# Group statistics of a second layer: from bn_stats on VectorE to accumulated activations on the scalar engine

## The chip, the cores and the metric

The kernel runs on one NeuronCore of one Trainium2 chip. The metric is the device time of one launch in microseconds; lower is better. Before the change three runs gave 3018.94 us at the median (3016.51 to 3023.95).

## The reference

The input x has 32 images of 32 channels of 128 x 128 numbers in fp32. Two layers run one after the other:

```
x = x + L0(gn(x))        # L0: matrix square root of each 128x128 channel, 5 Newton-Schulz steps
x = x + L1(gn(x), w1, w2)  # L1: 2-D Fourier transform, 32x32 low modes top and bottom
                           #     mixed over channels with w1 and w2, inverse transform, real part

def gn(v, G=16, eps=1e-5):     # per image and group of two channels
    g = v.reshape(B, G, C // G, H, W)
    m = mean(g, axis=(2, 3, 4)); s = var(g, axis=(2, 3, 4))
    return (g - m) / sqrt(s + eps)
```

The change touches the second gn alone: the mean and the variance of layer 1's input, over two channels of one image, 2 x 128 x 128 numbers. A Fourier transform is linear, so the kernel does not normalize layer 1's input. It transforms the raw values, multiplies the spectrum by 1 / sqrt(variance + eps), and corrects the one coefficient at frequency zero by the mean. So the statistics are needed only when an image's spectrum is finished.

## The kernel before

All data are fp32. The unit of work in layer 0 is a group of four channels of one image, a tile of 128 rows by 4 x 128 columns; an image has eight such groups, the launch 256. The square root of a channel is computed by a chain of matrix products on TensorE with short steps between them: VectorE combines a product with a tile, the scalar engine (ACT) copies or scales products out of PSUM, and GpSimd (POOL) subtracts from a scaled identity. There are two forms of the chain, "far" for images 1 to 18 and "near" for image 0 and images 19 to 31. The far form transposes on VectorE and puts the blocks together by four small DMAs from SyncE's queue; the near form transposes on TensorE.

The main loop counts rounds. In each round it visits eight lanes. A lane holds one group, written as a Python generator (`newton`); each visit runs the generator to its next `yield`, and so writes a few instructions into the engines' queues. A pause is a `yield` with no instruction. Nothing reorders what is written: the class `InOrder` keeps each engine's instructions in program order, so a round of the loop is a stretch of every engine's queue at once. A new group enters a free lane every 23/8 rounds in the far form and every 5 rounds in the near form. Next to the lanes there are queues of generators of which one step is taken at one place of each round: `norms` (scaling the input of coming groups), `preps` (layer 0's statistics of coming images, through `bn_stats`), `specs` (an image's layer 1 statistics and spectrum), `posts` (what follows a finished group), `prods` and `backs` (mixing products and inverse transforms of layer 1, for 20, 7, 3 and 2 images at a time). `posts` gets its step after the fourth lane. `step` works on the head of a queue, and when the head is exhausted goes on to the next at once.

A finished group is in the tile xt. `end` then appends `settle` to `posts`. `settle` stores xt to DRAM (`mid`), lets POOL fold its columns into a sum and a difference (tile fold), and takes the statistics of each pair of channels with VectorE's bn_stats, all in one step. After every four groups `forward` transforms the folded tiles on TensorE into u. After an image's eighth group `summed` is put on `specs`, and `spectrum` after it, so the second begins when the first has ended.

`bn_stats` writes six numbers for each partition, with a mean and a sum of squares about it for each of two halves. `summed` gets the group's statistics from these by way of `moments`: VectorE adds the half means, TensorE multiplies by avg_mean (a 128 x 128 matrix of one value, which sums over partitions and hands the sum to each of them), VectorE takes the differences from that mean, squares them and adds the rest. What comes out, two numbers for each of 16 groups, is widened from groups to channels (b_wide). Then four products with a 128 x 1 column avg_v sum it over partitions, each putting the 32 channels' variances on another 32 partitions of one PSUM tile, and a fifth gives the mean. A square root on ACT and one Newton step on VectorE give r, the factor by which ACT scales the spectrum.

PSUM has one pool of eight tiles (`bank`), taken in turn. xt has 14 buffers while the early ones exist, later 10; fold has three. ACT also issues the DMAs that load x, in two layouts, and the tiles for layer 0's statistics. Since every operation goes through a recording helper, the profile names line 89 for all of them, and its groups are told apart by their tiles.

Of the kernel before, what the change touches and what calls it, by code (L numbers as in the profile page):

```python
# [29 lines left out]
F32 = mybir.dt.float32  # L30
AF = mybir.ActivationFunctionType
ALU = mybir.AluOpType
AX = mybir.AxisListType
# [3 lines left out]
P = 128  # L37
B = 32
C = 32
G = 16  # L40
# [20 lines left out]
EPS = 1e-5  # L61
# [33 lines left out]
def conv_preact_kernel(  # L95
# [9 lines left out]
    nc = InOrder(tc)  # L105

    const = ctx.enter_context(tc.tile_pool(name="const", bufs=1))
# [10 lines left out]
    for n, f in (("v", EYE_V), ("q", EYE_Q)):  # L118
        e = const.tile([P, 1, P], F32, name=f"eye_{n}")
# [6 lines left out]
    avg_v = const.tile([P, 1], F32, name="avg_v")  # L126
    nc.vector.memset(avg_v, 0.5 / (P * P))
    avg_0 = const.tile([P, 1], F32, name="avg_0")
    nc.vector.memset(avg_0, -P * P / 256)


    mid = [dram.tile([P, C, P], F32, name=f"mid{b}", tag=f"mid{b}") for b in range(B)]
# [66 lines left out]
    def moments(st, ms, tag):  # L199

        n = st.shape[1]
        f = st.rearrange("p g (e t) -> p g e t", t=3)
        nc.vector.tensor_reduce(ms, f[:, :, :, 1], AX.X, ALU.add)
        yield from pause
        pm = bank()[:, 0, 0:n]
        nc.tensor.matmul(pm, avg_mean, ms, start=True, stop=True)
        nm = small.tile([P, n], F32, tag=f"{tag}_nm", name=f"{tag}_nm", bufs=2)
        nc.vector.tensor_scalar_mul(nm, pm, 2.0)
        d = small.tile([P, n, 2], F32, tag=f"{tag}_d", name=f"{tag}_d")
        nc.vector.tensor_tensor(  # L210
            d, f[:, :, :, 1], nm[:, :, None].to_broadcast([P, n, 2]), ALU.add
        )
        nc.vector.tensor_mul(d, d, d)
        nc.vector.scalar_tensor_tensor(d, d, 128.0, f[:, :, :, 2], ALU.mult, ALU.add)
        return nm, d
# [267 lines left out]
    def settle(b, g, st, xt):  # L483

        kept(nc.sync.dma_start(out=mid[b][:, 4 * g : 4 * g + 4, :], in_=xt))
        if g % 2 == 0:
            folds[b, g // 2] = sets.tile([P, 8, P], F32, tag="fold", name=f"fold{b}_{g}", bufs=3)
        f = folds[b, g // 2][:, 4 * (g % 2) : 4 * (g % 2) + 4, :]
        for half, op in enumerate((ALU.add, ALU.subtract)):
            nc.gpsimd.tensor_tensor(  # L490
                f[:, :, 64 * half : 64 * half + 64], xt[:, :, 0:64], xt[:, :, 64:128], op
            )
        for j in range(2):
            at = 8 * (g // 2 % 2) + 4 * (g // 4) + 2 * (g % 2) + j
            nc.vector.bn_stats(
                st[:, at, :], xt[:, 2 * j : 2 * j + 2, :].rearrange("p c h -> p (c h)")
            )
        settled.append(rounds)
        yield
# [35 lines left out]

    def summed(b, st):

        mq = small.tile([P, 2, G], F32, tag="b_mq", name=f"b_mq{b}")
        _, d = yield from moments(st, mq[:, 0, :], "b")
        yield  # L540

        nc.vector.tensor_reduce(mq[:, 1, :], d, AX.X, ALU.add)
        wide = small.tile([P, 2, G, 2], F32, tag="b_wide", name=f"b_wide{b}")
        nc.vector.tensor_copy(wide, mq[:, :, :, None].to_broadcast([P, 2, G, 2]))
        wide = wide.rearrange("p k g c -> p k (g c)")
        yield from pause
        pv = bank()[:, 0, :]
        for i in range(4):
            rows = slice(C * i, C * i + C)
            nc.tensor.matmul(pv[rows, 0:1], wide[:, 1, :], avg_v, start=True, stop=True)  # L550
        nc.tensor.matmul(pv[0:C, 1:2], wide[:, 0, :], avg_0, start=True, stop=True)
        v = small.tile([P, 2], F32, tag="b_v", name=f"b_v{b}")
        nc.vector.tensor_scalar(v[:, 0:1], pv[:, 0:1], 1.0, EPS, ALU.mult, ALU.add)
        nc.vector.tensor_copy(v[0:C, 1:2], pv[0:C, 1:2])
        yield
        s = small.tile([P, 3], F32, tag="b_r", name=f"b_r{b}")
        nc.scalar.activation(s[:, 0:1], v[:, 0:1], AF.Sqrt)
        yield
        nc.vector.reciprocal(s[:, 1:2], s[:, 0:1])
        nc.vector.tensor_scalar(  # L560
            s[:, 2:3], v[:, 0:1], s[:, 1:2], s[:, 1:2], ALU.mult, ALU.mult
        )
        nc.vector.tensor_scalar(s[:, 2:3], s[:, 2:3], -0.5, 1.5, ALU.mult, ALU.add)
        r = small.tile([P, 1], F32, tag="b_inv", name=f"b_inv{b}")
        nc.vector.tensor_mul(r, s[:, 1:2], s[:, 2:3])
        scales[b] = v, r
        yield
# [425 lines left out]
    made = {}  # L993
# [34 lines left out]
    def end(b, g, xt):  # L1028

        if g == 0:  # L1030
            u = up.tile([P, 2, 8, 2, L], F32, tag="u", name=f"u{b}")
            st = small.tile([P, G, 6], F32, tag="b_st", name=f"b_st{b}", bufs=2)
            ended[b] = (u, st)
        u, st = ended[b]
        posts.append(settle(b, g, st, xt))
        if g == C // 4 - 1:
            posts.append(then(summed(b, st)))
        if g % 4 == 3:
            posts.append(forward(b, g // 4, u))
        if g == C // 4 - 1:  # L1040
            posts.append(last(b, u))
# [144 lines left out]
```

## Time and profile before

| | us |
|---|---|
| median of three runs | 3018.94 |
| the profiled execution | 3016.65 |
| its span, first to last instruction | 3014.7 |
| TensorE busy (matmul) | 2897.6 |
| VectorE busy | 2321.8 |
| POOL busy | 1995.8 |
| scalar engine busy | 1652.1 |
| bn_stats on xt, 512 of 413 ns | 189.6 |
| bn_stats for layer 0, 504 of 412 ns and 8 of 418 ns | 188.4 |
| granted TensorE clock, share of full speed | 0.987 |

The profile is of one execution. A row "A <- B" in the list of waits gives the time that engine A stood idle until B had finished something, how often, and the longest. In the table of stages each engine has its busy time in the stretch and the number of its instructions. PE is TensorE's matmul side and PEld its weight loads, which overlap; DVE is VectorE and SP is SyncE. An fp32 product shows as two records, so a group's four products are eight. Tiles are named without their buffer numbers: ps is PSUM, and the names in `settle` and `summed` appear as b_st, b_mq, b_d, b_nm, b_wide, b_v, b_r and b_inv.

### The profile page before, as it was taken

How to read it: one execution, taken by the hardware profiler on the slowest of the kernel's cores; microseconds unless marked ns; L12 is line 12 of the kernel's file. 1: busy time of each engine (PE TensorE's matmuls, PEld its weight loads, DVE VectorE, ACT ScalarE, POOL GpSimd, SP SyncE). 2: the span in 40 equal slices, each digit the busy share in tenths (PEclk: the TensorE clock that was granted, in tenths of full speed). 3: DMA queues.
4: the chain of work that ended last, by engine and by line, in shares of the span. 5: the costliest groups of instructions: out<-in, count | busy, mean ns of one | idle time of the engine just before them, and what ended most of it. 6: DMA issues, size and time to landing. Idle time of an engine off the chain costs nothing.

```text
span 3014.7 us, 73315 instructions
## 1 busy us (share of the span) xinstructions
PE 2897.6 (96%) x27112; PEld 2689.0 (89%) x27112; DVE 2321.8 (77%) x4262; ACT 1652.1 (55%) x4187; POOL 1995.8 (66%) x2308
## 2 busy tenths in 40 slices
PE   7999999999999999999999999999989999999995
PEld 7899999999999999999999889888878899888884
DVE  7778898989888888889876645777886767776564
ACT  4566666566565656566554445455544544665452
POOL 4676777777777767777765434787777763678352
PEclk9999999999999999999999999999999999999997
DMA  5465655556565656565633566777877737676576
GB/s 176 135 176 145 171 163 153 167 152 180 134 192 135 192 131 195 142 183 140 190 102 99 158 209 208 257 247 254 271 235 245 252 121 225 203 242 216 175 230 242
DMA packets 442482, 560.91 MB, mean 186 GB/s; under 512 B 99344, under 2 KB 260112, under 8 KB 442128
## 3 DMA queue, kind: packets, MB, share of 16 engines
q1 hardware_dynamic: 328512, 347.77, 38.7%
q10 hardware_dynamic: 113616, 208.45, 22.2%
q8 instruction: 218, 3.57, 0.5%
q14 instruction: 136, 1.11, 0.1%
HBM read 326.93 MB, written 153.62 MB: 159 GB/s over the span
## 4 chain that ended last, share of the span: by engine, by line
PE 71%; POOL 8%; DVE 7%; DMA 7%; issue 5%; SPq 1%; ACT 1%; ACTq 0%; POOLq 0%; DVEq 0%
PE ps L89 71%; POOL yt L89 3%; POOL r L89 2%; POOL x L89 1%; POOL fold L89 1%; DMA yt<-mid 1%; SPq L89 1%; DVE turn L89 1%; DVE root L89 1%; DMA w<-turn 1%; DMA out<-yt 1%; DVE v L89 1%; DVE yt L89 1%; DVE a_d L89 1%; DMA xs<-in_xs 1%
## 5 line engine op out<-in xcount | busy, mean ns | idle before, releaser
L89 PE MATMUL ps<-my,q 128*128 128x128 f32 (+1 forms) x4096 | 747.0, 330 | 16.6 <-DVE q L89 9.9
L89 PEld LDWEIGHTS ps<-my,q 128*128 128x128 f32 x4096 | 623.0, 192 | 67.7 <-issue 7.4
L89 PE MATMUL ps<-w,v 128*128 128x128 f32 x4096 | 555.4, 279 | 19.6 <-DVE w L89 15.3
L89 ACT ACTIVATE b<-b,a_off,a_sc 128x128 f32<-128x128 f32 x1024 | 469.7, 491 | 166.2 <-issue 57.0
L89 ACT ACTIVATE my<-ps 128x512 f32<-128x512 f32 x512 | 306.2, 599 | 428.3 <-PE ps L89 408.9
L89 POOL TENSOR_TENSOR fold<-xt 128x256 f32<-128x256 f32 x512 | 363.4, 731 | 261.5 <-DVE xt L89 248.9
L89 PEld LDWEIGHTS ps<-w,v 128*128 128x128 f32 x4096 | 502.9, 193 | 32.5 <-DVE w L89 13.9
L89 POOL TENSOR_TENSOR yt<-yt,d 128x512 f32<-128x512 f32 x244 | 306.5, 1279 | 223.2 <-ACT d L89 195.5
L89 ACT ACTIVATE t<-ps 128x256 f32<-128x256 f32 x512 | 192.0, 381 | 311.7 <-PE ps L89 298.4
L89 DVE STREAM_TRANSPOSE turn<-v 128x512 f32<-128x512 f32 x288 | 326.1, 1132 | 9.9
L89 POOL TENSOR_SCALAR x<-xt,a_nm,a_sc 128x128 f32<-128x128 f32 x736 | 321.4, 450 | 15.6 <-DVE a_sc L89 15.4
L89 POOL TENSOR_TENSOR mb<-eye_q,mb 128x512 f32<-128x512 f32 x144 | 184.0, 1278 | 197.8 <-ACT y L89 139.2
L89 ACT ACTIVATE y<-ps,a_t_s 128x128 f32<-128x128 f32 x1024 | 290.4, 374 | 0.0
L89 POOL TENSOR_TENSOR v<-eye_v,x 128x512 f32<-128x512 f32 x144 | 184.0, 1278 | 143.8 <-ACT x L89 136.7
L89 PE MATMUL ps<-q,t 128*128 128x128 f32 x2048 | 273.9, 277 | 4.3 <-ACT t L89 3.7
L89 PE MATMUL ps<-x,b 128*128 128x128 f32 x2048 | 277.7, 279 | 0.0
L89 PE MATMUL ps<-x,q 128*128 128x128 f32 x2048 | 274.7, 277 | 3.0 <-DVE w L89 2.0
L89 DVE SCALAR_TENSOR_TENSOR v<-ps,v 128x512 f32<-128x512 f32 x288 | 195.1, 678 | 104.5 <-PE ps L89 101.8
L89 PE MATMUL ps<-y,t 128*128 128x128 f32 x2048 | 274.5, 277 | 0.1
L89 PE MATMUL ps<-my,mb 128*128 128x128 f32 x2048 | 272.2, 276 | 0.0
L89 PEld LDWEIGHTS ps<-my,mb 128*128 128x128 f32 x2048 | 257.9, 192 | 9.6 <-issue 1.6
L89 PEld LDWEIGHTS ps<-x,q 128*128 128x128 f32 x2048 | 249.4, 192 | 14.1 <-issue 8.4
(131 smaller groups left out, 5074.9 us busy)
## 6 DMA issues: line engine op xcount, KB each, us to landing
w<-turn SPq DMA_DIRECT2D x1152, 64.0 KB
b<-in_x ACTq DMA_DIRECT2D x256, 256.0 KB
xt<-in_xt ACTq DMA_DIRECT2D x256, 256.0 KB
mid<-xt SPq DMA_DIRECT2D x256, 256.0 KB
yt<-mid SPq DMA_DIRECT2D x128, 512.0 KB
xs<-in_xs ACTq DMA_DIRECT2D x252, 256.0 KB
out<-yt SPq DMA_DIRECT2D x115, 512.0 KB
plain<-in_wk SPq DMA_DIRECT2D x34, 512.0 KB
```

The costliest lines, as they stand in the source:

```text
L89: return self.tc.keep_in_program_order(issue(*args, **kw))
```

## The change

The second layer's statistics are gathered in another way. Layer 0's mean of each group is known from `prep` (a_nm, its negative). For each pair of channels `settle` now runs two activations on ACT over the 128 x 256 numbers: a Copy whose accumulated output is their sum per partition, and a Square with layer 0's negative mean as bias, whose accumulated output is the sum of squares about that mean. Their elementwise results go to one tile, waste, that nobody reads. A `yield` stands between the two pairs, so `settle` takes two rounds instead of one. bn_stats on xt is gone.

`summed` no longer calls `moments`. It widens sums, squares and layer 0's mean to channels (three VectorE copies, two of them for the mean's order of groups). For each of the four blocks of 32 partitions TensorE makes three products: the squares with avg_v, and the sum with avg_v and the mean with avg_s accumulated into one column, which gives the distance between the new mean and layer 0's. A product with avg_0 gives the mean as before, with another constant. On channels VectorE then takes the square of that distance off the mean of squares and adds eps. From there on nothing differs. The product with avg_mean and one of the two pauses of `summed` go; the statistics tile is 128 x 2 x 16 instead of 128 x 16 x 6, and a_nm has three buffers instead of two, since `summed` reads it late. `moments` itself stays, for layer 0.

```diff
-    nc.vector.memset(avg_0, -P * P / 256)
+    nc.vector.memset(avg_0, -0.5)
+    avg_s = const.tile([P, 1], F32, name="avg_s")
+    nc.vector.memset(avg_s, 1 / P)
+    waste = const.tile([P, 2 * P], F32, name="waste")
...
-        nm = small.tile([P, n], F32, tag=f"{tag}_nm", name=f"{tag}_nm", bufs=2)
+        nm = small.tile([P, n], F32, tag=f"{tag}_nm", name=f"{tag}_nm", bufs=3)
...
+        at = 8 * (g // 2 % 2) + 4 * (g // 4) + 2 * (g % 2)
         for j in range(2):
-            at = 8 * (g // 2 % 2) + 4 * (g // 4) + 2 * (g % 2) + j
-            nc.vector.bn_stats(
-                st[:, at, :], xt[:, 2 * j : 2 * j + 2, :].rearrange("p c h -> p (c h)")
+            if j:
+                yield
+            of = xt[:, 2 * j : 2 * j + 2, :].rearrange("p c h -> p (c h)")
+            n = 2 * g + j
+            nc.scalar.activation(
+                waste, of, AF.Copy, accum_out=st[:, 0, at + j : at + j + 1]
+            )
+            nc.scalar.activation(
+                waste,
+                of,
+                AF.Square,
+                bias=made[b][0][:, n : n + 1],
+                accum_out=st[:, 1, at + j : at + j + 1],
             )
...
-        mq = small.tile([P, 2, G], F32, tag="b_mq", name=f"b_mq{b}")
-        _, d = yield from moments(st, mq[:, 0, :], "b")
-        yield
-
-        nc.vector.tensor_reduce(mq[:, 1, :], d, AX.X, ALU.add)
-        wide = small.tile([P, 2, G, 2], F32, tag="b_wide", name=f"b_wide{b}")
-        nc.vector.tensor_copy(wide, mq[:, :, :, None].to_broadcast([P, 2, G, 2]))
+        wide = small.tile([P, 3, G, 2], F32, tag="b_wide", name=f"b_wide{b}")
+        nc.vector.tensor_copy(wide[:, 0:2], st[:, :, :, None].to_broadcast([P, 2, G, 2]))
+        for half in range(2):
+            nm = made[b][0].rearrange("p (a h c) -> p h a c", a=2, h=2)[:, half]
+            nc.vector.tensor_copy(
+                wide[:, 2, 8 * half : 8 * half + 8].rearrange("p (a c) e -> p a c e", a=2),
+                nm[:, :, :, None].to_broadcast([P, 2, 4, 2]),
+            )
...
             nc.tensor.matmul(pv[rows, 0:1], wide[:, 1, :], avg_v, start=True, stop=True)
+            nc.tensor.matmul(pv[rows, 2:3], wide[:, 0, :], avg_v, start=True, stop=False)
+            nc.tensor.matmul(pv[rows, 2:3], wide[:, 2, :], avg_s, start=False, stop=True)
         nc.tensor.matmul(pv[0:C, 1:2], wide[:, 0, :], avg_0, start=True, stop=True)
-        v = small.tile([P, 2], F32, tag="b_v", name=f"b_v{b}")
-        nc.vector.tensor_scalar(v[:, 0:1], pv[:, 0:1], 1.0, EPS, ALU.mult, ALU.add)
+        v = small.tile([P, 4], F32, tag="b_v", name=f"b_v{b}")
+        nc.vector.tensor_copy(v[:, 2:3], pv[:, 2:3])
         nc.vector.tensor_copy(v[0:C, 1:2], pv[0:C, 1:2])
+        nc.vector.tensor_scalar(v[:, 3:4], v[:, 2:3], v[:, 2:3], -1.0, ALU.mult, ALU.mult)
+        nc.vector.tensor_scalar(v[:, 0:1], pv[:, 0:1], EPS, v[:, 3:4], ALU.add, ALU.add)
...
-            st = small.tile([P, G, 6], F32, tag="b_st", name=f"b_st{b}", bufs=2)
+            st = small.tile([P, 2, G], F32, tag="b_st", name=f"b_st{b}", bufs=2)
```

## The prediction

> **What bounds the kernel now.** I read the engine totals first, then the 40 slices, then busy time by stage, then who waits for whom on TensorE and on the scalar engine, and last the timeline round the places that the edit touches.
>
> From the page, the totals and three rows of slices:
>
> ```profile
> PE 2897.6 (96%) x27112; PEld 2689.0 (89%) x27112; DVE 2321.8 (77%) x4262; ACT 1652.1 (55%) x4187; POOL 1995.8 (66%) x2308
> ...
> PE   7999999999999999999999999999989999999995
> ...
> DVE  7778898989888888889876645777886767776564
> ACT  4566666566565656566554445455544544665452
> ```
>
> TensorE is full nearly everywhere; VectorE comes second, at eight to nine tenths in the first half. The same by stage (span, then PE, PEld, DVE, ACT, POOL busy, clock, DMA share, GB/s), once in the far stage (images 1 to 18) and once in the near stage:
>
> ```profile
> 700.00:1000.00 300.00, 298.50 (x2506) 282.96 (x2505) 259.38 (x456) 181.66 (x464) 217.28 (x239) 1.00 0.57 157
> ...
> 2000.00:2300.00 300.00, 284.34 (x2540) 255.88 (x2538) 234.25 (x417) 154.88 (x406) 228.31 (x262) 0.99 0.75 247
> ```
>
> In the far stage TensorE idles 1.5 of 300 us, in the near stage 15.7. So VectorE's 86% does not set the pace: what is taken from it can return only what TensorE waits for it. Those waits, over the whole span, are these (total, times, longest):
>
> ```profile
> PE ps L89 <- DVE w L89: 18.2, 12, 3.2
> PE ps L89 <- DVE a_ms L89: 11.5, 1, 11.5
> PE ps L89 <- DVE q L89: 11.2, 15, 5.1
> PE ps L89 <- ACT my L89: 9.3, 7, 4.1
> ...
> PE ps L89 <- DVE b_wide L89: 4.4, 5, 1.5
> PE ps L89 <- DVE a_d L89: 4.2, 9, 1.0
> PE ps L89 <- DVE b_mq L89: 3.8, 1, 3.8
> ```
>
> With the smaller rows of that answer (v 2.2, xt 1.1, b_st 0.8, yt 0.5, b_v 0.3) TensorE waits 58.2 us for VectorE. Of this the 11.5 us for a_ms is the first image's statistics, which stay; 46.7 us can be touched, and 9.0 of them (b_wide, b_mq, b_st) belong to the chain that is rewritten.
>
> The room on the engine that gets the work, in the far stage, from its waits between 700 and 1000 us:
>
> ```profile
> ACT my L89 <- PE ps L89: 52.0, 44, 3.6
> ACT t L89 <- PE ps L89: 25.4, 40, 1.5
> ACT mb L89 <- PE ps L89: 9.4, 11, 1.3
> ACT b L89 <- issue: 5.0, 14, 1.3
> ```
>
> With z (3.3) the scalar engine waits 90 us for TensorE: time that other work can fill. The other 28 us of its idle time hang on transfers that it issues and on other engines, and are not free. The stage finishes 29 groups of four channels in these 300 us (58 bn_stats on xt, two a group), one in 10.3 us; so a group leaves 3.1 us free there.
>
> **What the Trainium skill says.** "ScalarE: Activation LUTs", section "What ACT_TABLE_LOAD costs", prices an ACTIVATE at 186 ns + 0.833 ns an element with immediates and 280 ns with one pointer operand. The trace agrees: 128x256 copies out of PSUM (z) take 380 ns against 399, the 128x128 scaling with one pointer (y) 374 against 387. Its section "Table sets" counts cheap functions as present in every set; whether Square is one no run shows yet, but the built program keeps one table load, as before. "TensorE: Matmul & The Clock Gate", section "LDWEIGHTS", lets a load grow with its columns; the trace agrees, 109 ns for 32 columns against 192 for 128. "Perfetto Trace Analysis", section "Matmuls", has PSUM banks rotate so that an evacuation overlaps the next matmuls; here eight banks do, and that rotation is where a late scalar engine would hurt.
>
> **The change part by part**, against the profiled execution: 3016.65 us around a span of 3014.7. The median of the three shown is 3018.94, 2.3 higher, so my sum is put on that.
>
> 1. *Statistics leave VectorE.* 512 bn_stats take 189.6 us; the old chain's two reductions 11.4, b_nm 5.2, the three b_d steps 13.4 + 10.7 + 18.6: 249 us. New are two small copies into b_wide, one more copy from PSUM and a product per image; by b_wide's mean of 461 ns (upper end, its median is 218) and b_r's 273 and 135 ns rows about 1.1 us each image, 35 us. Net about -214 us, to 70%. Gain: not those 214 but a part of the 46.7. The chain's own waits fall by 5 of 9.0. The largest is in the tail, where avg_mean waited 3.84 us for b_mq and b_wide held TensorE 1.50 more; one of the two round trips goes, but the first wait is mostly a yt load that stays (DVE idle 4.60 us before yt), so about 2 us come from there. Of the other 37.7, mostly w and q in the near stage, I take a quarter, 9: they are mostly late chains of PE, POOL and transfers, not a VectorE queue. Both ends: 0 and 25.
>
> 2. *Statistics arrive on the scalar engine.* Each group gets two steps, in two successive rounds of the main loop. A step is a Copy (z row: 0.38 us) and a Square with one pointer (y row 0.374 + 128 x 0.833 ns = 0.48). The Square waits for the Copy, since both write waste, so these two don't overlap. Writing the accumulator out is not in this trace: nothing at one end, at the other what a whole 128x1 ACTIVATE costs here, 0.197 us (b_r). I take 0.1. A step is 1.06 us (0.86 to 1.25), a group 2.1 (1.7 to 2.5), all 256 some 543 us (440 to 640): ACT to 73%. That is below the 3.1 us free of a far group, so the mean load fits. What counts is whether an evacuation behind a step comes too late. In the timeline of one group the both-products start at 708.35 and their scaling is done at 713.1; eight allocations later (y, fold, w, ident, w, my, q and the next) their banks are written again from 715.30: 2.8 us to spare. t, done 712.07, is read at 715.30 (3.2), y, done 713.1, at 723.04, mb done 723.5 is read at 727.45 (4). One step ahead of them is covered, two with a burst of b and x scalings and a transfer's issue are about the limit. I put in half a step, 0.55 us, for one group in seven: 256 / 7 x 0.55 = 20 us. This is the softest term: 0 to 60.
>
> 3. *More small matmuls.* Per image five small products become thirteen, in records ten become 26, and the 128x16 product with avg_mean (two records) goes. In the far stage the old ones look like this (start, duration):
>
> ```profile
> 729.33 0.24 PE L89 MATMUL ps<-avg_v,b_wide 128*32 128x1 f32 x8
> 729.41 0.20 PE L89 MATMUL ps<-avg,b_wide 128*32 128x1 f32 x2
> 729.55 1.16 PE L89 MATMUL ps<-x,b 128*128 128x128 f32 x8
> 730.54 0.31 PE L89 MATMUL ps<-a_ms,avg_mean 128*128 128x32 f32 x2
> 730.68 0.58 PE L89 MATMUL ps<-w,v 128*128 128x128 f32 x3
> ```
>
> Ten move the queue by 0.22 us, 22 ns each; a pair with avg_mean by 0.14. So 16 x 0.022 - 0.14 = +0.21 us an image, x 32 = +7. If each had to wait for its 109 ns load: 16 x 0.109 - 0.14 = 1.6, x 32 = +51. Pairs already follow each other in the same columns without that, so I take 7; TensorE is full, nothing hides it.
>
> 4. *Moved.* settle now takes two rounds, so posts need 20 steps an image instead of 12, with 23 rounds there (2.875 a group): no backlog. The fold matmuls, spectrum and the mid stores slide by a round against the lanes; summed has three steps fewer. On ACT the b and xt loads and xs prefetches (0.33 to 0.5 us to issue) stand behind a step now and then; they are issued groups ahead. The Copy waits for xt from VectorE, at least a round after it was issued (about 3.5 us in the far stage), and bn_stats before xt's reuse is no longer waited for. POOL gets the far b subtraction ahead of fold in places. Zero, hidden by the prefetch distance; without that cover a transfer's issue, 0.4 us a group, 100 us.
>
> Sum: -5 - 9 + 20 + 7 = +13, 3029.7 for the profiled execution; 3018.9 + 13 = 3032 us for the median.
>
> **Rivals.**
> - *The scalar engine becomes the far stage's bound.* For: with 2.5 us a group only 0.6 of the free 3.1 is left, its work comes in bursts (the stretch from 749.6 to 754.7 us is solid), and spectrum adds 2 us once an image. Against: VectorE ran at 86% without stopping TensorE. It decides where a step passes 1.55 us, or where bursts cost 3 us an image: 3 x 18 = 54 in the far stage, 9 in the rest (part 2's share for 112 of 256 groups), 7 from part 3, less 14: +56, near 3075.
> - *Both engines hide it.* Steps fit, the +7 is met by the waits that go: 3019, same.
> - *Faster*, the other side: less VectorE queueing lifts w and q in the near stage and prep's a_d, half of 46.7 us goes, less the 7 of part 3 with ACT at zero: -16, so about 3002. It decides once VectorE's relief beats TensorE's extra records and all ACT delays together. For: w and q waits are named after VectorE, and its small operations stretch there (b_d 1.06 us at one place). Against: they are a few long waits, 3.2 and 5.1.
>
> **How the numbers follow.** A few units in a thousand, 0.3% or 9 us, is what can be told from no change. The likeliest case, 3032 (own range 3022 to 3048), has 0.43, of which about 0.31 lies over 3028; ACT as bound 0.23; both hidden 0.15; faster 0.19. Slower: 0.31 + 0.23 = 0.54; same 0.12 + 0.15 = 0.27; faster 0.19. For eight in ten I leave out the lower half of the faster case and the upper half of the bound one: 3001 to 3085.
>
> **What would show it.** VectorE near 70%, ACT near 73%, with 1024 ACTIVATEs to waste of about 0.38 and 0.48 us and, beside them, whatever reads the accumulator; PE's idle time in 700 to 1000 us still under 3 us and its waits for ACT (my, t, mb) up from 9.3 by 10 to 30 us; b_wide's records at 22 ns steps. If ACT waits for PE vanish in the far stage, or PE's idle passes 8 us in 300, the bound rival holds. If near-stage waits for w and q fall by more than 15 us with ACT's unchanged, the faster one does. The prediction is wrong if the accumulator costs more than 0.4 us, or if small products in one column group serialize.

## The result and the profile after

The changed kernel takes 3056.86 us at the median of four runs (3053.35 to 3058.76), the kernel before 3018.43 (four runs, 3016.51 to 3023.95). The ratio is 1.0123, with a 95% interval of 1.0105 to 1.0140: 38 us slower. The profiled execution took 3055.6 us around a span of 3053.8, 39.1 more span than before.

The page of the kernel after, engine totals and three rows of slices, as before:

```profile
PE 2909.0 (95%) x27560; PEld 2689.4 (88%) x27560; DVE 2148.8 (70%) x3687; ACT 2121.6 (69%) x6235; POOL 1998.6 (65%) x2308
...
PE   7999999999999999999999999999999999999995
...
DVE  7778786878777787878775644776676665676554
ACT  4778777777777777777776656666666666777663
```

VectorE lost 173 us and is no longer at nine tenths; the scalar engine gained 470 us and stands at seven tenths through the far stage. TensorE's row looks the same, and the 39 us are in it: its busy time grew by 11.4 us and its idle time by 27.7, from 117.1 to 144.8. The stages of the kernel after (span, then PE, PEld, DVE, ACT, POOL busy, clock, DMA share, GB/s) say where:

```profile
700.00:1000.00 300.00, 292.79 (x2481) 276.48 (x2481) 235.39 (x383) 229.29 (x688) 212.73 (x234) 0.99 0.55 154
...
2000.00:2300.00 300.00, 280.63 (x2534) 251.64 (x2533) 219.92 (x373) 189.63 (x567) 230.47 (x263) 0.99 0.73 245
```

In the far window TensorE idles 7.2 us instead of 1.5. Over all of 150 to 1600 us its idle time rose from 7.2 to 41.5, while from 1600 to 2960 it fell from 65.8 to 50.9. The windows are fixed in time, so they don't hold quite the same work in both kernels; but the loss is plainly in the far stage, which was nearly gapless before. POOL's fold of the 152nd group, the last far one, starts at 1580.6 us before and at 1622.5 after, so the whole loss is there by then. What TensorE waits for there, between 150 and 1600 us (total, times, longest), first before the change, then after:

```profile
PE ps L89 <- DVE a_d L89: 3.3, 8, 0.4
PE ps L89 <- DVE q L89: 2.8, 9, 0.3
PE ps L89 <- ACT my L89: 1.1, 2, 0.8
```

```profile
PE ps L89 <- ACT my L89: 12.8, 9, 2.5
PE ps L89 <- DVE q L89: 12.7, 14, 1.5
PE ps L89 <- ACT b L89: 7.1, 15, 1.6
PE ps L89 <- ACT t L89: 6.2, 5, 2.1
PE ps L89 <- ACT z L89: 2.4, 1, 2.4
```

That is 1.1 us for ACT and 6.1 for VectorE before, 28.5 and 12.7 now. These are few waits, the longest of 2.5 us, not a steady one. The new groups themselves, from the groups of instructions by shape (count, then busy us and mean ns, then idle before them):

```profile
L89 ACT ACTIVATE waste<-xt,a_nm 128x256 f32<-128x256 f32 x512 | 260.4, 509 | 16.6
L89 ACT ACTIVATE waste<-xt 128x256 f32<-128x256 f32 x512 | 217.5, 425 | 23.1 <-DVE xt L89 6.7 <-DMA yt<-mid 4.8 <-DMA out<-yt 3.8
L89 ACT ACTIVATION_READ_ACCUMULATOR waste<-xt 128x1 f32 x512 | 104.7, 205 | 0.0
L89 ACT ACTIVATION_READ_ACCUMULATOR waste<-xt,a_nm 128x1 f32 x512 | 95.5, 186 | 0.0
```

Each accumulated output is read out by an instruction of its own, 205 and 186 ns. The instructions of a step overlap at their ends: from the Copy's start to the start of the next operation 1.03 to 1.08 us pass in most steps that another operation follows at once (median 1.06).

One of the stalls shows how it comes about. The timeline of the scalar engine in the kernel after (start, duration, operation, and in brackets the idle time before it and what ended it; ACTq is its queue issuing a transfer):

```profile
513.54 1.14 ACT L89 ACTIVATE y<-ps,a_t_s 128x128 f32<-128x128 f32 x4
516.78 1.86 ACTq L89 DMA_DIRECT2D xs<-in_xs  x3
518.69 0.49 ACT L89 ACTIVATE b<-b,a_off,a_sc 128x128 f32<-128x128 f32 x1 [4.02 <-DMA w<-turn]
519.09 0.48 ACT L89 ACTIVATE x<-xt,a_off,a_sc 128x128 f32<-128x128 f32 x1
519.48 0.48 ACT L89 ACTIVATE b<-b,a_off,a_sc 128x128 f32<-128x128 f32 x1
519.86 0.40 ACT L89 ACTIVATE waste<-xt 128x256 f32<-128x256 f32 x1
520.17 0.19 ACT L89 ACTIVATION_READ_ACCUMULATOR waste<-xt 128x1 f32 x1
520.39 0.51 ACT L89 ACTIVATE waste<-xt,a_nm 128x256 f32<-128x256 f32 x1
520.80 0.19 ACT L89 ACTIVATION_READ_ACCUMULATOR waste<-xt,a_nm 128x1 f32 x1
520.89 0.48 ACT L89 ACTIVATE x<-xt,a_off,a_sc 128x128 f32<-128x128 f32 x1
521.28 0.48 ACT L89 ACTIVATE b<-b,a_off,a_sc 128x128 f32<-128x128 f32 x1
521.42 0.33 ACTq L89 DMA_DIRECT2D xs<-in_xs  x1
521.66 0.57 ACT L89 ACTIVATE my<-ps 128x512 f32<-128x512 f32 x1
```

and TensorE at the same time:

```profile
518.94 1.09 PE L89 MATMUL ps<-fold,tab 128*32 128x504 f32 x12
522.29 2.08 PE L89 MATMUL ps<-my,q 128*128 128x128 f32 x8 [2.26 <-ACT my L89]
524.16 1.72 PE L89 MATMUL ps<-my,mb 128*128 128x128 f32 x8
525.71 1.06 PE L89 MATMUL ps<-x,q 128*128 128x128 f32 x8
```

After y the scalar engine's next entries are three loads of xs. The first can't be issued for 2.1 us, and getting all three out takes 1.9 more: the engine does no other work for 4.02 us. Then it works off b, x, b, the new Copy and Square (1.03 us), x, b, and only then the evacuation my that TensorE needs; TensorE has stood for 2.26 us. Without the step my could have been a microsecond earlier.

A load that isn't ready stops the engine it is issued from: "DMA: Bandwidth & Descriptors" of the Trainium skill, section "Anatomy of one DMA — SWDGE (gpsimd) path", follows a transfer that GpSimd issues and says that a transfer's wait is made on the issuing sequencer ahead of dispatch, not in the DMA engine. This trace agrees for the scalar engine: in those 4.02 us nothing else of it runs. Such holds are not new. The kernel before plus nothing but an empty pause (experiment e5 below, faster than the kernel before) has one just as long, in its timeline of the scalar engine:

```profile
705.96 0.44 ACTq L89 DMA_DIRECT2D b<-in_x  x1
709.65 0.33 ACTq L89 DMA_DIRECT2D xt<-in_xt  x1
710.03 0.88 ACT L89 ACTIVATE b<-b,a_off,a_sc 128x128 f32<-128x128 f32 x2 [4.24 <-DMA w<-turn]
710.81 0.48 ACT L89 ACTIVATE x<-xt,a_off,a_sc 128x128 f32<-128x128 f32 x1
...
711.58 0.63 ACT L89 ACTIVATE t<-ps 128x256 f32<-128x256 f32 x2
```

and its stage says that TensorE never stopped:

```profile
700.00:1000.00 300.00, 300.00 (x2524) 284.85 (x2523) 257.12 (x462) 183.97 (x473) 219.45 (x242) 1.00 0.58 160
```

With four microseconds lost and no step in the way, the evacuations were still in time. That is the suspicion which the experiments test.

### The profile page after: what moved, and what is told of

Read it like the earlier page. It is cut to its first block, busy times and chain, and to the rows that moved or that the text cites. A ratio compares the mean times of both kernels' runs of the same rounds, so it can differ in the third digit from the quotient of the medians.

```text
span 3053.8 us, 75754 instructions
## 1 busy us (share of the span) xinstructions
PE 2909.0 (95%) x27560; PEld 2689.4 (88%) x27560; DVE 2148.8 (70%) x3687; ACT 2121.6 (69%) x6235; POOL 1998.6 (65%) x2308
## 4 chain that ended last, share of the span: by engine, by line
PE 64%; DMA 9%; DVE 7%; POOL 7%; issue 5%; ACT 4%; SPq 2%; ACTq 1%; DVEq 0%; POOLq 0%
PE ps L89 64%; POOL yt L89 3%; DMA w<-turn 3%; DMA yt<-mid 2%; POOL r L89 2%; SPq L89 2%; POOL x L89 2%; DVE turn L89 1%; ACT b L89 1%; DMA xs<-in_xs 1%; POOL fold L89 1%; DVE v L89 1%; DMA out<-yt 1%; ACTq L89 1%; DVE q L89 1%
## 5 line engine op out<-in xcount | busy, mean ns | idle before, releaser
L89 ACT ACTIVATE t<-ps 128x256 f32<-128x256 f32 x512 | 184.8, 379 | 221.7 <-PE ps L89 214.0
L89 DVE SCALAR_TENSOR_TENSOR w<-ps,r 128x512 f32<-128x512 f32 x224 | 153.3, 684 | 174.8 <-POOL r L89 87.7
```

The source lines that it names most:

```text
L89: return self.tc.keep_in_program_order(issue(*args, **kw))
```

## The experiments

The theories when they began: the scalar engine's steps delay evacuations (the prediction's part 2 and its bound rival), against a cost of the new `summed` with its small products, or of the moved work, since `settle` takes two rounds. Medians below are of four or more runs where nothing else is said, and each ratio is to the kernel before, run beside it (its median lay between 3014.86 and 3022.22 in these comparisons).

### Which part of the change costs

e1 is the kernel before with only the pause between the two pairs:

```diff
         for j in range(2):
+            if j:
+                yield
             at = 8 * (g // 2 % 2) + 4 * (g // 4) + 2 * (g % 2) + j
             nc.vector.bn_stats(
```

> The kernel before with one edit: a yield between the two bn_stats of a group, so that settle takes two rounds as it does after the change. Nothing else is changed. Theory A (the scalar engine's queue is late because of the added activations) and theory C (the added small matmuls in summed): no change, 3012 to 3025 us. Theory B (the second round of settle moves fold, forward and the stores to worse places): most of the 38 us, 3040 to 3057.

e2 is the kernel after without the four activations; b_st is set to a constant once an image, so layer 1's statistics are left out:

```diff
-            nc.scalar.activation(waste, of, AF.Copy, accum_out=st[:, 0, ...])
-            nc.scalar.activation(waste, of, AF.Square, bias=..., accum_out=st[:, 1, ...])
...
             st = small.tile([P, 2, G], F32, tag="b_st", name=f"b_st{b}", bufs=2)
+            nc.vector.memset(st, 16.0)
```

> The kernel after without the four activations of each group; the statistics tile is set to a constant once an image, so layer 1's statistics are left out and its normalization is by a constant. The two rounds of settle, the new summed and VectorE's relief stay. Theory A: the loss goes, and VectorE's relief shows: 3008 to 3022, with TensorE's idle time in the far stage back under 3 us in 300. Theory B: 3045 to 3057. Theory C: 3045 to 3057 too, as its matmuls stay.

e3 is the kernel before with the pause and with the same activations beside bn_stats, their sums going to tiles that nobody reads; `summed` is the old one, VectorE is not relieved:

```diff
...
+            if j:
+                yield
...
             nc.vector.bn_stats(
                 st[:, at, :], xt[:, 2 * j : 2 * j + 2, :].rearrange("p c h -> p (c h)")
             )
...
+            nc.scalar.activation(waste, of, AF.Copy, accum_out=idle[:, 0, at : at + 1])
+            nc.scalar.activation(waste, of, AF.Square, bias=made[b][0][:, n : n + 1],
+                                 accum_out=idle[:, 1, at : at + 1])
```

> The kernel before with settle in two rounds and, after each bn_stats, the same Copy and Square with accumulated outputs, to tiles that nobody reads. VectorE keeps its bn_stats and the old summed is used; only scalar work is added. Theory A: as slow as after the change or slower, since VectorE isn't relieved: 3045 to 3075. Theory B: as e1_split. Theory C: 3012 to 3025.

Measured:

| kernel | median us | ratio (95%) |
|---|---|---|
| e1, pause alone | 3000.67 | 0.9929 (0.9906 to 0.9952) |
| e2, all but the activations | 2997.60 | 0.9919 (0.9887 to 0.9951) |
| e3, pause and activations, bn_stats stays | 3050.27 | 1.0096 (1.0075 to 1.0116) |
| the change | 3056.86 | 1.0123 (1.0105 to 1.0140) |

The activations cost 3050.27 - 3000.67 = 50 us where nothing else differs, and 3056.86 - 2997.60 = 59 us on top of the rest of the change. The rest of the change together is 22 us faster than the kernel before, and the pause alone gives 19 of them. So neither the new `summed` nor the moved work costs: the moved work gains, which none of the three expectations had. The measured 38 is about 59 less 20. In the traces of e2 and the kernel after, 58 us of span apart, TensorE waits 34.5 and 72.5 us for ACT over the whole span, 38 more, and is busy 16.6 us longer.

### What the gain of the pause is, and what VectorE's relief is worth

e5 leaves both bn_stats together and puts an empty pause behind them. In the program's order all queues but VectorE's are the same as in e1; only the second of the two bn_stats stands a round earlier.

```diff
                 st[:, at, :], xt[:, 2 * j : 2 * j + 2, :].rearrange("p c h -> p (c h)")
             )
+        yield
         settled.append(rounds)
         yield
```

> The kernel before with one more yield at the end of settle and nothing in it: forward, the next settle and the statistics of the image come a round later, as in e1_split, but both bn_stats of a group still stand together. e1_split was 19 us faster than before. Theory D (the gain is from where forward and fold come to stand): as e1_split, 2995 to 3007. Theory E (the gain is from VectorE's 0.74 us of bn_stats cut in two, so that what stands behind is later by less): as before, 3013 to 3024.

e8 is e1 without the 512 bn_stats on xt (b_st set to a constant once an image; layer 1's statistics are left out).

> e1_split without bn_stats on xt (the statistics tile is set to a constant once an image, so layer 1's statistics are left out): VectorE's relief of 190 us alone, with the old summed. By the prediction's part 1 the relief is worth about 9 us: 2988 to 2996. If it is worth nothing because TensorE is full: 2997 to 3004. Against e2_no_act, 2998, it gives the price of the new summed, predicted +7 less 5.

e7 is the kernel after without its pause, so that all four activations come in one round.

> The kernel after without the yield between the two pairs of activations, so settle takes one round and the scalar engine gets 2.2 us at once instead of twice 1.1. If the yield's 19 us of gain is there in the changed kernel too, and longer bursts make evacuations later: 3070 to 3100. If only one of the two: 3060 to 3075. If neither: 3050 to 3060.

e5 took 2997.58 us (0.9940, 0.9918 to 0.9962). Dividing VectorE's burst has nothing to do with the gain: a round's delay of what follows `settle` (the transform of the folded tiles, `summed`, `spectrum`) is the gain. e8 took 3005.43 (0.9954, 0.9929 to 0.9979), no faster than e1. VectorE lost 150 us of work there (2295.0 to 2143.8 us busy), and nothing came of it. e7 took 3063.12 (1.0147, 1.0126 to 1.0168), 6 us above the change, though the intervals overlap: two bursts of two activations cost at most slightly less than one of four, and the pause's 19 us are not simply kept when the activations are there.

### Which images

e4 uses bn_stats and the old `summed` for the far images in one round, the activations and the new `summed` for the near ones. g15 is e4 with e5's empty pause for the far images.

```diff
         for j in range(2):
+            if is_far(b):
+                nc.vector.bn_stats(st[:, at + j, :], ...)
+                continue
             if j:
                 yield
...
+        if is_far(b):
+            yield                      # this pause in g15 alone
         settled.append(rounds)
...
```

> Both ways in one kernel: the 18 far images take bn_stats and the old summed in one round of settle, the 14 near images the activations and the new summed. The loss lay in the far stage by the stage tables (34 of 39 us), where the scalar engine had 3.1 us free a group against 5.5 or so in the near stage. Theory A: 3010 to 3026, the far stage as full as before. Theory C: 14 of 32 images' matmuls, about 3034. If near images lose too, 3026 to 3040.

> A candidate: far images with bn_stats and the empty step of e5_empty_step, near images with the activations and the new summed, as in e4_near_only. If both gains are of different stages and add: 2988 to 2997. If the empty step's gain is in the near images or at the end: 3003 to 3015.

e4 took 3014.05 us (0.9979, 0.9969 to 0.9990; 20 runs), g15 3004.99 (0.9962, 0.9948 to 0.9976; five runs). The pause in the far images is worth 9 us of medians between these two, though their intervals against the kernel before overlap. Against e5, the same program with bn_stats everywhere, the activations of the near images cost 7 us (2 in a thousand by the ratios, whose intervals overlap as well). By subtraction the other 50 or so are the far images'; no run has the activations there alone, but the traces agree: POOL's fold of the 152nd group, the last far one, starts at 1579.3 us in e2 and at 1622.5 in the kernel after, 43 us apart. What the pause gains besides those 9 us is not settled.

### How much of a step fits

e6 keeps both activations but takes no accumulated output, so a step takes 0.87 us instead of 1.06 (medians, from the Copy's start to the next operation's). g12 keeps the Copy with its accumulator alone, 0.41 us a step. e6 leaves out layer 1's statistics, g12 its variance; b_st, or its second half, is set to a constant once an image.

```diff
-            nc.scalar.activation(waste, of, AF.Copy, accum_out=st[:, 0, ...])
-            nc.scalar.activation(waste, of, AF.Square, bias=..., accum_out=st[:, 1, ...])
+            nc.scalar.activation(waste, of, AF.Copy)                  # e6
+            nc.scalar.activation(waste, of, AF.Square, bias=...)      # e6
+            nc.scalar.activation(waste, of, AF.Copy, accum_out=...)   # g12, nothing else
```

> The kernel after with the same Copy and Square but without accumulated outputs, so the 1024 reads of the accumulator (200 us of the 478 us added to the scalar engine) go; the statistics tile is set to a constant once an image, so layer 1's statistics are left out. Theory A, if the loss goes with the scalar engine's time: e2_no_act to after is 59 us for 478, so 278 leave 34: about 3031, 3022 to 3040. Theory A, if only the last part of the load hurts (room runs out): 3000 to 3020. If instead the place of the steps counts and not their length: 3045 to 3057.

> The kernel after with the Copy of each step and without the Square; the sums of squares are set to a constant, so the variance of layer 1's input is left out. A step falls from 1.1 us to about 0.6. Against e2_no_act (no activations, 2998) and after (3057): in proportion to the scalar engine's time half of the 59 us is left, 3022 to 3035. If the loss is made by evacuations that just miss their slack, the first half costs less than the second: 3002 to 3021. If each step costs by standing there, whatever its length: over 3040.

| step | kernel | ACT busy us | median us | ratio (95%) | TensorE's waits for ACT, 150 to 1600 us |
|---|---|---|---|---|---|
| none | e2 | 1653.1 | 2997.60 | 0.9919 (0.9887 to 0.9951) | 3.4 |
| 0.41 us | g12 | 1840.9 | 3001.90 | 0.9948 (0.9929 to 0.9968) | 13.8 |
| 0.87 us | e6 | 2035.5 | 3053.28 | 1.0111 (1.0093 to 1.0130) | 28.7 |
| 1.06 us | after | 2121.6 | 3056.86 | 1.0123 (1.0105 to 1.0140) | 28.5 |

The first 0.41 us cost about 4 us in all (9 by the ratios, and their intervals overlap), the next 0.46 about 50. In proportion to the scalar engine's busy time g12 would have lost 24 us and e6 48. So the small dose costs less than its share: there is room, and it ends somewhere between these two. Three doses don't show how abruptly, and that there is room at all rests on g12 alone. The accumulator's read is not what costs; without it the kernel is no faster to speak of. Nor does it hold the engine for long: e6 is busy 86 us less than the kernel after, not the 200 that its expectation counted for the reads, since they overlap their neighbours.

### Whether the loads in the same queue take the room

Loads of b, xt and xs stand in the scalar engine's queue, a third of them xs. g13 is the kernel after without the xs loads of images 1 to 31 (bn_stats for layer 0 reads one tile of image 0 that is held, so those images' layer 0 statistics are left out); g14 is e5 with the same cut, as its control.

```diff
+    held = []
...
-        for k in range(ahead):
-            load(k)
+        if first_b:
+            tiles.extend([held[0]] * len(parts))
+        else:
+            for k in range(ahead):
+                load(k)
+            held.append(tiles[0])
...
-            if k + ahead < len(parts):
+            if not first_b and k + ahead < len(parts):
                 load(k + ahead)
```

> The kernel after without the loads of the tiles for layer 0's statistics of images 1 to 31: bn_stats reads one tile of image 0 again and again, so these statistics are left out. A third of the loads in the scalar engine's queue goes, and no other queue gets them. To be read against g14_empty_no_xs. Theory F (loads that wait in that queue make the activations' steps late): the two differ by clearly less than the 59 us of after against e2_no_act or e5_empty_step, 10 to 40 us, and TensorE waits less for the scalar engine in the far stage than 28.5 us. Theory A (the time of the activations alone): by 50 to 65 us.

> e5_empty_step with the same loads left out, the control for g13_after_no_xs. TensorE is full in e5_empty_step's far stage, so little changes: 2985 to 3000.

| | with xs loads | without |
|---|---|---|
| no activations | 2997.58 (e5) | 2981.98 (g14; 0.9882, 0.9864 to 0.9901) |
| activations | 3056.86 (after) | 2995.24 (g13; 0.9929, 0.9912 to 0.9945) |
| their price | 59 | 13 |

The same activations that cost 59 us cost 13 where a third of the loads is gone. The page of g13 shows that the scalar engine does just as much as in the kernel after:

```profile
PE 2891.9 (97%) x27560; PEld 2681.6 (90%) x27560; DVE 2153.2 (72%) x3687; ACT 2122.5 (71%) x6235; POOL 1999.0 (67%) x2308
```

and of TensorE's waits between 150 and 1600 us, ACT is gone altogether. This row is the whole list:

```profile
PE ps L89 <- DVE q L89: 11.6, 11, 1.5
```

The next table sets the holds beside the waits. It counts from the scalar engine's timeline, between 150 and 1600 us, the idle stretches of 2 us and more that something other than TensorE ended (layer 0's square root, which waits for VectorE once in each preparation, is left out):

| kernel | activations | long holds, us | TensorE's waits for ACT |
|---|---|---|---|
| before | no | 11, 30 | 1.1 |
| e5 | no | 9, 26 | 3.3 |
| e2 | no | 31, 91 | 3.4 |
| g13 | yes | none | 0 |
| g12 | Copy alone | 23, 83 | 13.8 |
| e3 | yes | 20, 65 | 25.8 |
| e6 | yes, no accumulator | 33, 99 | 28.7 |
| after | yes | 27, 82 | 28.5 |

Each of the 27 long holds of the kernel after has a load's issue in it, as has each of e2's 31; the issuing itself takes 27 of the 82 us. Long holds alone (e2) leave TensorE 3.4 us of waits for ACT, activations alone (g13) none, both together 28.5. Two reservations: the cut in g13 and g14 also takes traffic away (the DMA share between 150 and 1600 us falls from 0.56 to 0.49) and VectorE's waits for xs. The second can't be what costs: between 150 and 1600 us VectorE waits 51.6 us for xs in e2, which has no loss, and only 15.6 in e3, which has the whole of it. For the first, the next runs leave the traffic and move the loads instead. And e2 has no activations and as many long holds as the kernel after, so it isn't they that make the holds; why e2 has three times as many as e5 the runs don't say.

### Moving the loads to the other queue

e9 is the kernel after with the loads of b and xt, and of xs from image 1 on, issued by SyncE; e11 is e5 with the same. e10 moves xs alone.

```diff
-            kept(nc.scalar.dma_start(out=t, in_=src))                                  # xs: e9, e10, e11
+            kept((nc.sync if first_b else nc.scalar).dma_start(out=t, in_=src))
...
-        kept(nc.scalar.dma_start(out=t, in_=x[b, :, 4 * g : 4 * g + 4, :]))            # e9, e11
-        kept(nc.scalar.dma_start(out=xt, in_=xt_in[b, :, 4 * g : 4 * g + 4, :]))
+        kept(nc.sync.dma_start(out=t, in_=x[b, :, 4 * g : 4 * g + 4, :]))
+        kept(nc.sync.dma_start(out=xt, in_=xt_in[b, :, 4 * g : 4 * g + 4, :]))
```

> The kernel after with the loads of x in both layouts and of the tiles for layer 0's statistics issued by SyncE's queue instead of the scalar engine's (image 0's statistics tiles stay). The activations stay. Theory F (each load waits in the scalar engine's queue for a buffer or for an earlier transfer to land, 2 to 4 us at a time, and with the added steps behind it the evacuations come too late; without the steps the queue caught up): TensorE's waits for the scalar engine in the far stage, 28.5 us after the change, fall under 8 and the time to 3000 to 3022. Theory A (the scalar engine's time alone, or the place of the steps): 3045 to 3060. If the loads hold up SyncE's small transfers instead, its waits for w appear and nothing is won.

> e5_empty_step (bn_stats on VectorE, one empty step at the end of settle, 2998 us) with the same loads issued by SyncE's queue. Theory F: without the added activations the scalar engine catches up after each load anyway, so nothing is to be won: 2990 to 3003. If loads on the scalar engine cost time in every kernel, 2970 to 2988, and then e9 says nothing on the change. If SyncE's queue suffers: over 3005.

> The same for the statistics tiles alone, a third of the loads. Theory F: a part of the way, 3020 to 3045. Theory A: 3050 to 3060.

e9 took 3045.87 us (1.0078, 1.0052 to 1.0104), e11 3052.11 (1.0100, 1.0076 to 1.0125), e10 3056.94 (1.0119, 1.0084 to 1.0154). Between e11 and e9 the activations cost nothing (-6 us, the intervals overlap). But the move itself cost 54 us (e5 to e11). TensorE's largest waits between 150 and 1600 us in e9, where none for ACT is left:

```profile
PE ps L89 <- DVE q L89: 30.0, 23, 2.1
PE ps L89 <- DVE v L89: 9.1, 10, 1.7
```

The wait has changed its name. Why q and v are late there is not separated: SyncE's transfers of w, from which they are made, now share a queue with the loads, and VectorE, which makes them, waits 135.0 us for xs, against 61.3 in the kernel after (124.5 in e11, 15.0 in e5). e10, with the xs loads alone on SyncE, came out even with the change, where its expectation had put it if the time of the activations alone counted. Its trace says something else than its time: TensorE's waits for ACT fell from 28.5 us to 0.7, with no transfer taken away, and waits for VectorE's q (25.4), xt (11.6) and v (10.1) stand in their place. It has no control without activations, so their price there is not known. So e9 and e10 say that without these loads in its queue the scalar engine is in time, but another bound stands at the same height, which makes their times the weaker evidence beside g13 and g14.

### What the loads wait for

A load in the scalar queue waits for its tile to come free, and, in the program as built, for one of eight semaphores that the transfers of both queues use in turn; that can be a w transfer of SyncE, and w<-turn is what 14 of the 27 long holds of the kernel after name (3 of 31 in e2). e16 and e17 tried to tell these apart by asking for xs one tile later, e16 in the kernel after, e17 in e5:

```diff
-        ahead = 3 if first_b else 8
+        ahead = 2 if first_b else 8
```

> The kernel after with the statistics tiles loaded two ahead instead of three: with four buffers a load then follows bn_stats on its old tile by two steps of the statistics instead of one, so it finds its buffer free. The loads still wait in the scalar engine's queue for the earlier transfer on their DMA semaphore. If the waits for buffers made the steps late: 3005 to 3035. If the waits for earlier transfers (the eight semaphores, taken in turn by both queues): 3045 to 3060.

> e5_empty_step (2998 us) with the same shorter lead, the control: 2990 to 3003 if the lead matters little there; slower, 3005 or more, if tiles now come too late for bn_stats.

e16 took 3084.42 us (1.0223, 1.0202 to 1.0244), e17 3021.27 (1.0006, 0.9991 to 1.0020; 12 runs). The activations still cost 63 us, and both kernels lost over 20: VectorE waited in the far stage 70.9 us (e17) and 109.1 us (e16) for xs, against 15.0 in e5 and 61.3 in the kernel after. A shorter lead makes the tiles late and hides what it was to show.

The traces themselves tell the two apart, for they keep with every load the semaphores that it waits for and the one that it will raise. In all 27 long holds of the kernel after, in all 31 of e2 and all 9 of e5, the longest standstill (48 of the 82 us in the kernel after) ends with a wait for the very semaphore that the load will raise, so for the transfer that used it last. In the kernel after that was one of SyncE's 27 times: 17 times w<-turn, 7 times xs<-spec, 3 times mid<-xt. In 16 of the 27 the load has no wait for an engine at all; in the other 11, which also wait for an engine to free the tile, it goes out within 0.1 us of that semaphore. In the hold shown above the first load of xs waits for the semaphore of an xs<-spec transfer that SyncE issued 5.5 us before, the third for that of a w<-turn issued 2.5 us before. So these holds are waits for the shared semaphores. No run gives the loads semaphores of their own, so what that would win is not known.

### What is best

e5 (2997.58 us, 0.9940) and e1 (3000.67 us, 0.9929) compute all that the reference asks for and beat both kernels, by about 20 and 60 us. Each adds a pause and nothing else to the kernel before.

## Why the prediction was right or wrong

The sign and the range held; the size did not, 13 us forecast against 38 measured.

- **Part 1, VectorE's relief, -14: wrong.** VectorE came to 70% as said, but e8 took 150 us off it and e1 with all of them was no slower. The argument that w and q waits are late chains and no VectorE queue was right and should have been taken to its end: nothing, not a quarter. In the kernel after TensorE's waits for q in the far stage even rose, from 2.8 to 12.7 us.
- **Part 2, the price of a step: right.** 1.06 us forecast, a median of 1.06 seen. ACT came to 69%, not 73%, since it is busy only 470 us longer: a step's instructions overlap each other and their neighbours. Fear of a dear accumulator was unfounded; it has an instruction of its own, and in e6 leaving it out saves 4 us of medians, within the spread.
- **Part 2, "half a step, 0.55 us, for one group in seven = 20 us": the step that failed.** Its measured value is 50 us (e3 against e1) to 59 (after against e2). The slack of 2.8 to 4 us was read off a timeline with no hold in it, and the 28 of 118 us that were set aside as "not free" were treated as an even tax. A part of such idle time, in the whole far stage 30 of 143 us before and 82 of 160 after, comes as single holds of 2 to 4.5 us, some longer than the slack, and the step falls into the catching up after one. The room was right on average and wrong where it counted: 0.41 us of step fit into it, 0.87 no longer did. The stated ends, 0 to 60, do hold the 59.
- **Part 3, small products, +7: the price right, its effect not seen.** In the far stage the 26 records run from 654.74 to 655.29 us, 21 ns each. In the whole, e2 with them (2997.60) is no slower than e8 without (3005.43).
- **Part 4, "Zero, hidden by the prefetch distance": wrong, twice.** A load that is asked for ahead of its reader still stopped the engine that issues it, here by the wait for its semaphore, and 46 of the 59 us go where the xs loads go (g13 and g14). And the second round of `settle`, set at nothing, is worth -19 (e1) to -20 us (e5).

Put together from the runs: about -20 for the pause, +59 for the activations, nothing measurable for the rest, +39.

The signs named beforehand: TensorE's waits for my, t and mb were to rise from 9.3 us by 10 to 30. The 9.3 was my alone; with t (3.7) it was 13.0, and it rose to 46.4, by 33, slightly more than forecast; its idle time in 700 to 1000 us was to stay under 3 and was 7.2. The bound rival was to hold if it passed 8, which it did between 400 and 700 us and again between 1300 and 1600, with 9.6 each. So the measured time lies about halfway between the forecast and that rival. But ACT's waits for TensorE did not vanish: in the far stage it still has 174 us of them (434 before). The engine had time left over; it came too late at certain places. The faster rival's ground, that VectorE's load was what made w and q late, falls with e8. That both engines hide it falls with the 50 to 59 us that the activations cost.

## What to carry to other kernels

The room that an in-order engine had for more work in this kernel was not its idle time, nor its mean wait for the bound engine, but what was left at the worst places, after a long hold in its own queue. Transfers issued from that queue made the holds, each by waiting for a semaphore that the other queue's transfers use too; the names of the waits alone didn't tell that, the semaphores did. Test the room by dose: here a little of the new work was nearly free and a little more cost nearly everything, so splitting or thinning the step tells more than its total. And before work is shifted to another engine, try moving only its place in the order; here an empty pause was worth more than taking 150 us off the second busiest engine, which was worth nothing.

## What the hardware showed

A stall can cost more than its length. After the wait of 2.26 us shown above the next eight records (four products) took 2.08 us and eight more 1.72, where 1.06 is usual. The granted clock of that kernel, in short windows before, in and behind this place and at two other waits, of 1.55 us (ended at 1052.69) and of 2.50 us (ended at 1520.56; columns as in the stages, the clock third from the end):

```profile
518.00:522.00 4.00, 2.03 (x22) 1.22 (x20) 1.67 (x4) 3.27 (x10) 0.48 (x1) 1.00 0.87 270
522.00:526.00 4.00, 3.71 (x19) 3.71 (x20) 3.38 (x9) 2.27 (x7) 2.02 (x2) 0.57 0.36 104
526.00:530.00 4.00, 4.00 (x30) 3.79 (x30) 3.50 (x4) 2.09 (x7) 3.98 (x5) 1.00 0.61 189
...
1054.00:1058.00 4.00, 4.00 (x16) 3.52 (x15) 3.09 (x6) 2.67 (x9) 4.00 (x5) 0.58 0.67 188
...
1520.00:1524.00 4.00, 3.44 (x30) 3.44 (x31) 3.10 (x7) 3.07 (x9) 3.54 (x3) 1.00 0.54 182
1524.00:1528.00 4.00, 4.00 (x31) 3.79 (x30) 3.19 (x5) 2.85 (x10) 3.52 (x6) 1.00 0.63 187
```

The clock fell to 0.57 in the four microseconds after the wait and was back at 1.00 in the next four. The far stage of this kernel has three more such drops, behind waits of 1.46, 1.55 and 2.42 us, and none behind waits of 1.84, 1.88, 2.10 and 2.50 us. e6 has one behind 2.29 us (0.59 in 193 to 197 us) and one about its wait of 4.58 us (0.50 in 1513 to 1517 us); e2's far stage has none. "TensorE: Matmul & The Clock Gate" of the Trainium skill, section "What's actually happening", describes this halving after an idle window of about 3.4 us; here a wait of 1.46 us was followed by it in one place and one of 2.50 us was not in another, so the length of a single wait doesn't decide it. It is a small part of the loss: four microseconds at 0.57 lack 1.7 us of clock, four such drops 6.8. By this estimate they may make up 7 of the 16.6 us by which TensorE's busy time, 2892.4 us in e2, is longer in the kernel after (2909.0); no run separates that, and the rest is not explained.
